# Shifting a few more edge chunks from GpSimd gathers to row-by-row loads in a graph layer

## The chip, the cores and the metric

The kernel runs on one core of one Trainium2 chip. The metric is device time in microseconds (us) of one execution. Three runs of the kernel before gave a median of 2628.38 us (2608.38 to 2629.09). One more execution was recorded by the hardware profiler; it took 1931.2 us. All views of the profile below belong to that one execution.

## What is computed

A graph network layer on 12,500 nodes with 128 features and 200,000 edges, sorted by destination. The reference, cut to what matters:

```python
h = jnp.maximum(_layernorm(x, axis=-1), 0.0)
msgs = h[src]
agg = jax.ops.segment_sum(msgs, dst, num_segments=n)
deg = jax.ops.segment_sum(jnp.ones((src.shape[0],)), dst, num_segments=n)
agg = agg / jnp.maximum(deg, 1.0)[:, None]
z = jax.nn.relu(agg @ Wg + h @ Ws + bg)
z = jnp.tanh(z @ W1 + b1)        # 128 -> 512
z = jnp.tanh(z @ W2 + b2)        # 512 -> 512
return x + z @ W3 + b3           # 512 -> 128
```

Everything is float32.

## The kernel before

**Setup (lines 132 to 323).** The normalised rows `h` are computed in pieces of up to 14 tiles of 128 nodes and written to a table `htab` in device memory (line 246). The edge indices are turned so that each edge chunk has a column.

**Chunks.** The edges are cut into 1563 chunks of 128. For each chunk the 128 source rows must lie in one SBUF tile of 128 x 128. `add` (line 432) then multiplies this tile with a one-hot matrix of the destinations (built on VectorE in groups of eight chunks, `onehot`, line 374), which adds the rows into a PSUM window of 144 nodes. Since the edges are sorted, chunk c falls around node 8c. There are three ways to get the rows of a chunk:

- 80 chunks are "raw": their rows of `x` are gathered by GpSimd during setup (line 153), before `htab` is complete, and normalised afterwards.
- 38 chunks are "slow" (the lists `slow_s` and `slow_a`, lines 86 to 100). Their rows are read from `htab` one at a time, 512 bytes each, by ordinary DMAs whose address comes from a register. 23 are read by SyncE (`srows`), 15 by ScalarE (`arows`). `row_loads` (line 337) first loads 32 addresses into registers (line 344, one table load per 32 rows) and then issues the 32 DMAs. The tiles come from the pool `rows_one`, with two buffers for each name.
- The remaining 1445 chunks are gathered from `htab` by GpSimd, one indirect DMA per chunk (`gather`, line 308), into 32 buffers (`AHEAD`).

**Blocks.** The nodes are cut into blocks of 512 (the last ones are smaller). When all chunks of a block have been added, its layers follow (`part0` to `part4`, lines 526 to 593): matmuls on TensorE, ReLU, Tanh and Identity on ScalarE. Each block needs the nodes' own rows transposed: `own` (line 480) loads 512 rows of `htab` into the tile `hb` (one buffer) on SyncE, `own_turned` (line 489) transposes them on TensorE and has ScalarE copy the result to `hT`. `own_part` (line 500) loads the block of `x` for the residual, and the finished block is stored, both on SyncE.

**What sets the order.** TensorE, ScalarE and SyncE keep the order in which the program issues their work (`keep_in_program_order`). The loop over the chunks (line 642) interleaves it: a chunk is added, then perhaps one step of a block's layers. Row loads are dealt out there by the number of chunks passed: SyncE gets a batch of 32 rows for each 32/128 of `EACH` = 58 chunks, ScalarE four rows for each 4/128 of `EACH_A` = 76 chunks. So ScalarE's row loads stand between its activations, and SyncE's stand between the loads of `hb` and `xb` and the stores of `o`. Every DMA of SyncE and ScalarE also takes the next of eight completion semaphores that both engines share, and waits for the DMA that had this semaphore before.

The lines of the loop that deal out row loads and own rows:

```python
batch = behind * P // (EACH * LOADS)
if behind > SLOW0 - 2 * EACH and batch > (behind - 1) * P // (EACH * LOADS):
    next(loading, 0)
...
if c % span == span - 52:
    own(c // span + 1)
if c % span == span - 10:
    own_turned(c // span + 1)
```

`span` is 64 chunks, one block. The functions that the diff touches:

Of the kernel before, what the change touches and what calls it, by code (L numbers as in the profile page):

```python
# [22 lines left out]
F32 = mybir.dt.float32  # L23
# [8 lines left out]
P = 128  # L32
EPS = 1e-5
CPR = 16
BLK = 512
# [3 lines left out]
RAW0 = 256  # L39
STEP = 40  # L40
AHEAD = 32
SLOW0 = 120
EACH = 58
EACH_A = 76
TOGETHER = 4
LOADS = 32
LATE = 12
LEAD = 10
QUICK = 1376
# [11 lines left out]
def windowed(ctx, tc, x, src, dst, Wg, Ws, bg, W1, b1, W2, b2, W3, b3, out, flag):  # L61
    nc = tc.nc
    N, D = x.shape
# [18 lines left out]
    def raw(c):  # L82
        return RAW0 <= c < RAW1 and (c - RAW0) % STEP < GRP


    slow_s, slow_a = [], []
    ns, na = 0, EACH // 2
    for c in range(SLOW0, NCH - 12):
        if raw(c):
            continue  # L90
        if ns <= 0:
            slow_s.append(c)
            ns = EACH
        elif na <= 0 and c < QUICK:
            slow_a.append(c)
            na = EACH_A
        else:
            ns -= 1
            na -= 1
# [20 lines left out]
    dram = ctx.enter_context(tc.tile_pool(name="dram", bufs=1, space=bass.MemoryType.DRAM))  # L120
    const = ctx.enter_context(tc.tile_pool(name="const", bufs=1))
    raws = ctx.enter_context(tc.tile_pool(name="raws", bufs=1))
    rows_one = ctx.enter_context(tc.tile_pool(name="rows_one", bufs=2))
    rows_in = ctx.enter_context(tc.tile_pool(name="rows_in", bufs=AHEAD))
    ps_c = ctx.enter_context(tc.tile_pool(name="ps_c", bufs=1, space=PSUM))
    ps_a = ctx.enter_context(tc.tile_pool(name="ps_a", bufs=2, space=PSUM))
# [55 lines left out]
    def centre(pool, xt, k, stats):  # L182
        nc.vector.tensor_reduce(stats[:, 0], xt, AX.X, ALU.add)
        nc.vector.scalar_tensor_tensor(xt, spread(stats[:, 0], k), -1.0 / D, xt, op0=ALU.mult, op1=ALU.add)
        sq = pool.tile([P, k, D], F32, name=f"sq{k}")
        nc.scalar.activation(sq, xt, AF.Square)
        nc.vector.tensor_reduce(stats[:, 1], sq, AX.X, ALU.add)

    def factors(stats):
        nc.scalar.activation(stats[:, 1], stats[:, 1], AF.Sqrt, bias=eps, scale=1.0 / D)  # L190
        nc.vector.reciprocal(stats[:, 1], stats[:, 1])
# [98 lines left out]
    ml = ctx.enter_context(tc.tile_pool(name="ml", bufs=2))  # L290
# [14 lines left out]
    def sp_dma(*a):  # L305
        tc.keep_in_program_order(nc.sync.dma_start(*a))  # L306

    def gather(c):
        r = rows_in.tile([P, D], F32, name="rows")
        nc.gpsimd.indirect_dma_start(  # L310
            out=r, out_offset=None, in_=htab,
            in_offset=bass.IndirectOffsetOnAxis(ap=scol[:, c : c + 1], axis=0),
        )
        rows_t[c] = r
# [40 lines left out]
    def raw_stats(i):  # L355
        return stats_raw[:, :, i * GRP : (i + 1) * GRP]

    def raw_scaled(i):
        h = raw_rows[i]
        scale(h, h, GRP, raw_stats(i))  # L360
        for j in range(GRP):
            rows_t[RAW0 + i * STEP + j] = h[:, j]
# [11 lines left out]
    def onehot(g):  # L374
        k = min(GRP, NCH - g * GRP)
        lo, w = window(g * GRP)
        is_raw = raw(g * GRP)
        oh = ed.tile([P, GRP, W_RAW], F32, name="ohr", bufs=2) if is_raw else oh_bufs[g % OHS]
        if not is_raw and w < oh_w[g % OHS]:
            nc.vector.memset(oh[:, :, w : oh_w[g % OHS]], 0.0)  # L380
            oh_w[g % OHS] = w
        nc.vector.tensor_tensor(  # L382
            oh[:, :k, :w], lane[:, None, :w].to_broadcast([P, k, w]),
            dloc[:, g * GRP : g * GRP + k][:, :, None].to_broadcast([P, k, w]), op=ALU.is_equal,
        )
        ohs[g] = oh
        step, n = (oh.shape[2], w) if is_raw else (PITCH - per, w + per * (k - 1))
        cnt = ed.tile([P, PITCH], BF16, name="cnt", bufs=16)
        part, row, col = oh.ap
        shifted = bass.AP(tensor=oh.tensor, offset=oh.offset, ap=[part, [col[0], n], [step * col[0], k]])  # L390
        with nc.allow_low_precision(reason="whole numbers up to the chunks of a group"):
            nc.vector.tensor_reduce(cnt[:, :n], shifted, AX.X, ALU.add)  # L392
        counts[g] = (lo, n, cnt)
# [10 lines left out]
    def count(b):  # L404

        n, m = blocks[b]
        dg = flat(ps_m.tile([P, 4, P], F32, name="pm"))
        groups = sorted({c // GRP for c in reach[b]})
        for g in groups:
            lo, w, cnt = counts[g]  # L410
            a0, a1 = max(lo, n), min(lo + w, n + m)
            pe.matmul(
                dg[:, a0 - n : a1 - n], ones, cnt[:, a0 - lo : a1 - lo], start=(g == groups[0]), stop=(g == groups[-1]),
                skip_group_check=True,
            )
        rd = ml.tile([P, BLK], F32, name="rd", bufs=3)
        nc.vector.tensor_scalar(rd[:, :m], dg[:, :m], 1.0, None, op0=ALU.max)  # L417
        nc.vector.tensor_reduce(total[:, b : b + 1], dg[:1, :m], AX.X, ALU.add)
        nc.vector.reciprocal(rd[:, :m], rd[:, :m])  # L419
        rds[b] = rd  # L420
# [59 lines left out]
    def own(s):  # L480

        n0 = s * BLK
        n = min(BLK, N - n0)
        k = -(-n // P)
        hb = ml.tile([P, BLK // P, D], F32, name="hb", bufs=1)
        sp_dma(hb[:, :k], htab[n0 : n0 + k * P, :].rearrange("(t p) d -> p t d", p=P))
        owns[s] = hb

    def own_turned(s):

        k = -(-min(BLK, N - s * BLK) // P)
        hb = owns.pop(s)
        pt = ps_t.tile([P, BLK // P, P], F32, name="pt")
        for t in range(k):
            pe.transpose(pt[:, t, :], hb[:, t, :], ident)
        hT = ml.tile([P, BLK], F32, name="hT")
        act.copy(hT[:, : k * P], pt[:, :k, :].rearrange("p t n -> p (t n)"))
        hTs[s] = hT
# [116 lines left out]
    work, done, nxt, behind = [], 0, 0, 0  # L615
    ngrp = -(-NCH // GRP)
    span = BLK // per
    now = at = 0

    def store(upto):  # L620
        while stores and stores[0][0] <= upto:
            sp_dma(*stores.pop(0)[1:])
# [5 lines left out]
    def go_on(w):  # L628
        nonlocal now
        if w:  # L630
# [3 lines left out]
            if w[1] is None:  # L634
                work.remove(w)

    own(0)
    own_turned(0)
    onehot(0)
    onehot(1)  # L640
    counted = 0
    for c in range(NCH):
        g = c // GRP
        at = c
        store(c if c >= QUICK else c - LATE)
        if c % GRP == 0 and g + 2 < ngrp:
            onehot(g + 2)
            if raw((g + 2) * GRP):
                raw_scaled(((g + 2) * GRP - RAW0) // STEP)
            if 2 <= g < 2 + NRAW:  # L650
                centre(ed, raw_rows[g - 2], GRP, raw_stats(g - 2))
            if g == 2 + NRAW:
                factors(stats_raw)

        while c % GRP == GRP // 2 and counted < len(blocks) and reach[counted][-1] // GRP <= g + 1:
            count(counted)
            counted += 1
        while nxt < len(order) and nxt < behind + AHEAD:
            gather(order[nxt])
            nxt += 1  # L660
        if not raw(c) and c not in slow:
            behind += 1
            batch = behind * P // (EACH * LOADS)
            if behind > SLOW0 - 2 * EACH and batch > (behind - 1) * P // (EACH * LOADS):
                next(loading, 0)
            batch = behind * P // (EACH_A * TOGETHER)
            if behind > 48 and batch > (behind - 1) * P // (EACH_A * TOGETHER):
                next(loading_a, 0)
        if c >= QUICK:

            there = 7.5 + 1.251 * (NRAW * GRP + order.index(c)) if c not in slow else 0
            while soonest() and max(now, soonest()[2]) < there:
                go_on(soonest())
            now = max(now, there) + 0.27
        add(c)

        lead = LEAD if c < QUICK else 2
        if done < len(blocks) and (c - lead if across[done] else c) >= reach[done][-1]:
            if across[done]:
                merge(done)  # L680
            quick = reach[done][-1] + LEAD >= QUICK

            before = done - 1 if done and reach[done - 1][-1] + LEAD < QUICK else None
            work.append([layers(done, before), 0, 0, 0, quick and blocks[done][1] <= P])
            done += 1
        if (c // span + 1) * BLK < N:
            if c % span == span - 52:
                own(c // span + 1)
            if c % span == span - 10:
                own_turned(c // span + 1)  # L690
        if c < QUICK:
            if c % 2 == 0:
                go_on(work[0] if work else None)
        if c == QUICK:
            for b, (_, n) in enumerate(blocks):
                if n < BLK:
                    own_part(b)
# [379 lines left out]
```

## Time and profile before

| What | Value |
|---|---|
| Median of three runs | 2628.38 us (2608.38 to 2629.09) |
| Profiled execution | 1931.2 us |
| Its span, first to last instruction | 1928.7 us |
| What lies around the span | 2.5 us |
| TensorE matmul busy | 1299.0 us (67%), granted clock 0.866 |
| VectorE busy | 1066.8 us (55%) |
| ScalarE busy, without DMA issue | 228.1 us (12%) |
| GpSimd busy | 1442.0 us (75%) |
| DMA engines | 0.2 to 0.3 of their time after setup, 72 GB/s on average |

The profiled execution is 697 us shorter than the median of the runs. The profile can't show why; it is one execution, and each of its durations is taken as it stands.

How to read the profile: a row of a group names the line, the engine, the operation and the tiles it writes and reads ("out<-in"), the number of instructions, busy time, mean nanoseconds of one, and the idle time of the engine just before them with what ended most of it. A row of the waits names who waited for whom, the total in us, how many times, and the longest. A row of the timeline has a start, a duration and the number of merged instructions; in brackets the idle time before. "SPq" and "ACTq" are DMAs being issued by SyncE and ScalarE; issuing is not counted as busy. "Issue" is time in which nothing shown was waited for.

### The profile page before, as it was taken

Reading aid. Unit: us, or ns where it says so; the run is one execution under the profiler, and the core shown is the slowest. Engines: PE = TensorE matmul, PEld = TensorE weight load, DVE = VectorE, ACT = ScalarE, POOL = GpSimd, SP = SyncE. Lnnn points to the kernel's source line nnn. Section 1 sums busy time; section 2 is a strip of 40 time slices with the busy share of each in tenths; the row PEclk is TensorE's granted clock in tenths of the full one; section 3 lists DMA queues with packets and bytes.
Section 4 is the critical chain, followed back from the end, with each engine's and each line's share of the span. In section 5 each row is a group of like instructions: output and inputs, shape, how many; then the busy total and the mean of one; then the engine's idle time right before and its main releaser. Section 6 shows DMA issues by size and latency. Waiting matters only on the chain.

```text
span 1928.7 us, 24991 instructions
## 1 busy us (share of the span) xinstructions
PE 1299.0 (67%) x5212; PEld 819.1 (42%) x5212; DVE 1066.8 (55%) x651; ACT 228.1 (12%) x362; POOL 1442.0 (75%) x1533
## 2 busy tenths in 40 slices
PE   0056487775757678758775676566776746878787
PEld 0034354443535445534443344344443424554466
DVE  7964865555556856636544465354554536645430
ACT  1100111010101111111100110001101101101122
POOL 7777777777777777777777777777777777777774
PEclk9999688898878888888887898878988879879698
DMA  8822222222222222222222222222222222222221
GB/s 202 233 65 53 55 67 59 61 71 60 67 71 66 66 70 67 71 71 61 65 61 66 71 61 65 61 71 66 61 66 66 61 70 61 71 78 71 66 62 40
DMA packets 128692, 139.69 MB, mean 72 GB/s; under 512 B 35036, under 2 KB 103294, under 8 KB 128336
## 3 DMA queue, kind: packets, MB, share of 16 engines
q0 software_dynamic: 48800, 100.04, 20.5%
q1 hardware_dynamic: 72654, 33.65, 6.4%
q10 hardware_dynamic: 7076, 4.32, 0.9%
q14 instruction: 119, 0.97, 0.2%
q8 instruction: 43, 0.70, 0.2%
HBM read 125.07 MB, written 12.82 MB: 71 GB/s over the span
## 4 chain that ended last, share of the span: by engine, by line
DMA 31%; PE 28%; issue 17%; SPq 11%; DVE 5%; POOL 3%; ACTq 3%; ACT 1%; POOLq 0%; DVEq 0%
PE pm L297 16%; DMA rows<-htab,scol 16%; SPq L306 10%; PE agg L297 6%; DMA arows<-htab 5%; PE edge L297 4%; DMA srows<-htab 4%; POOL rows L310 3%; DMA hb<-htab 3%; ACTq L335 3%; DVE cnt L392 2%; DMA xt<-in_x_dram 2%; PE pt L300 1%; DVE oh L382 1%; SPq L344 1%
## 5 line engine op out<-in xcount | busy, mean ns | idle before, releaser
L310 POOL DMA_INDIRECT rows<-htab,scol x1445 | 1363.4, 944 | 440.8 <-issue 258.9
L297 PE MATMUL pm<-h,w 128*128 128x512 f32 (+4 forms) x1344 | 649.1, 580 | 26.3 <-ACT h L329 26.3
L297 PE MATMUL agg<-oh,rows 128*128 128x144 f32 (+3 forms) x2068 | 484.4, 342 | 219.9 <-DMA rows<-htab,scol 217.1
L297 PEld LDWEIGHTS agg<-oh,rows 128*128 128x128 f32 x2068 | 360.7, 215 | 530.1 <-DMA rows<-htab,scol 395.2
L382 DVE TENSOR_TENSOR oh<-shared,dloc 128x1152 f32<-128x1152 f32 (+2 forms) x186 | 243.4, 1314 | 605.8 <-PE edge L297 354.9
L392 DVE TENSOR_REDUCE cnt<-oh 128x200 bf16<-128x1600 f32 (+2 forms) x186 | 525.8, 2832 | 5.4
L297 PEld LDWEIGHTS pm<-h,w 128*128 128x128 f32 x1344 | 223.4, 206 | 42.2 <-ACT h L329 29.4
L297 PEld LDWEIGHTS edge<-oh,rows 128*128 128x128 f32 x822 | 150.3, 219 | 160.5 <-issue 85.8
L297 PE MATMUL edge<-oh,rows 128*128 128x144 f32 (+2 forms) x822 | 181.8, 333 | 39.7 <-DMA rows<-htab,scol 39.4
L300 PE MATMUL pt<-ident,hb 128*128 128x128 f32 x98 | 24.5, 398 | 242.7 <-DMA hb<-htab 242.7
L329 ACT ACTIVATE h<-pm,b2c 128x512 f32<-128x512 f32 (+4 forms) x112 | 70.8, 632 | 447.6 <-PE pm L297 229.3
L300 PEld LDWEIGHTS pt<-ident,hb 128*128 128x128 f32 x98 | 16.8, 204 | 246.3 <-issue 246.3
L153 POOL DMA_INDIRECT raw<-in_x_dram,rsrc x80 | 77.7, 971 | 25.4 <-issue 23.8
L329 ACT ACTIVATE h<-pm,b1c 128x512 f32<-128x512 f32 (+4 forms) x112 | 69.9, 632 | 203.2 <-PE pm L297 107.3
L419 DVE RECIPROCAL rd<-rd 128x512 f32<-128x512 f32 (+4 forms) x28 | 81.8, 2920 | 0.0
L332 ACT COPY hT<-pt 128x512 f32<-128x512 f32 (+1 forms) x25 | 14.4, 577 | 410.2 <-PE pt L300 383.9
L589 DVE TENSOR_TENSOR o<-pt,xb 128x512 f32<-128x512 f32 x23 | 15.8, 688 | 75.9 <-PE pt L300 75.9
L417 DVE TENSOR_SCALAR rd<-pm 128x512 f32<-128x512 f32 (+4 forms) x28 | 17.2, 616 | 63.1 <-PE pm L297 63.1
L212 PE MATMUL pm<-ident,idx_f 98*128 98x98 f32 x32 | 6.2, 376 | 62.0 <-DVE idx_f L208 55.7
L297 PE MATMUL pm<-mT,wg 128*128 128x512 f32 (+4 forms) x56 | 32.6, 669 | 22.7 <-DVE mT L533 22.5
L329 ACT ACTIVATE h<-pm,bgc 128x512 f32<-128x512 f32 (+4 forms) x28 | 17.7, 632 | 240.0 <-PE pm L297 144.1
L297 PE MATMUL pm<-hT,ws 128*128 128x512 f32 (+4 forms) x56 | 34.8, 711 | 0.0
(72 smaller groups left out, 496.9 us busy)
## 6 DMA issues: line engine op xcount, KB each, us to landing
srows<-htab SPq DMA_DIRECT2D x2944, 0.5 KB
arows<-htab ACTq DMA_DIRECT2D x1920, 0.5 KB
rows<-htab,scol POOLq DMA_INDIRECT x1445
hb<-htab SPq DMA_DIRECT2D x24, 256.0 KB
xb<-in_x_dram SPq DMA_DIRECT2D x23, 256.0 KB
out_dram<-o SPq DMA_DIRECT2D x23, 256.0 KB
htab<-h SPq DMA_DIRECT2D x6, 896.0 KB
xt<-in_x_dram SPq DMA_DIRECT2D x5, 896.0 KB
```

Of the source, the lines that this page charges most:

```text
L153: nc.gpsimd.indirect_dma_start(out=t[:, j, :], out_offset=None, in_=x, in_offset=bass.IndirectOffsetOnAxis(ap=rsrc[:, g, j : j + 1], axis=0),)
L297: tc.keep_in_program_order(nc.tensor.matmul(*a, **k))
L300: tc.keep_in_program_order(nc.tensor.transpose(*a, **k))
L306: tc.keep_in_program_order(nc.sync.dma_start(*a))
L310: nc.gpsimd.indirect_dma_start(out=r, out_offset=None, in_=htab, in_offset=bass.IndirectOffsetOnAxis(ap=scol[:, c : c + 1], axis=0),)
L329: tc.keep_in_program_order(nc.scalar.activation(*a, **k))
L335: tc.keep_in_program_order(nc.scalar.dma_start(*a))
L344: loads, vs = nc.values_load_multi_w_load_instructions(place[i : i + 1, p0 : p0 + LOADS], engines=[engine], min_val=0, max_val=(N - 1) * ROWB,
L382: nc.vector.tensor_tensor(oh[:, :k, :w], lane[:, None, :w].to_broadcast([P, k, w]), dloc[:, g * GRP : g * GRP + k][:, :, None].to_broadcas ...
L392: nc.vector.tensor_reduce(cnt[:, :n], shifted, AX.X, ALU.add)
L417: nc.vector.tensor_scalar(rd[:, :m], dg[:, :m], 1.0, None, op0=ALU.max)
L419: nc.vector.reciprocal(rd[:, :m], rd[:, :m])
```

## The change

The sync engine reads the rows of 27 chunks instead of 23 and ScalarE those of 19 instead of 15; GpSimd gathers 1437 chunks instead of 1445. Each of the two has four row buffers instead of two. The first slow chunk is chunk 160 instead of 120, and SyncE's batches are dealt out so that a chunk is read up to three intervals of 48 ahead instead of two of 58. ScalarE's last slow chunk may lie up to 60 chunks behind `QUICK`. The tile `hb` has two buffers; the load for a block is issued right after the transposes of the block before it, a whole block (64 chunks) ahead of its own transposes instead of 42 chunks. Setup reads the indices of 46 slow chunks (`at_i`, line 321) instead of 38.

```diff
-SLOW0 = 120
-EACH = 58
-EACH_A = 76
+SLOW0 = 160
+EACH = 48
+EACH_A = 60
...
-        elif na <= 0 and c < QUICK:
+        elif na <= 0 and c < QUICK + EACH_A:
...
-    rows_one = ctx.enter_context(tc.tile_pool(name="rows_one", bufs=2))
+    rows_one = ctx.enter_context(tc.tile_pool(name="rows_one", bufs=4))
...
-        hb = ml.tile([P, BLK // P, D], F32, name="hb", bufs=1)
+        hb = ml.tile([P, BLK // P, D], F32, name="hb", bufs=2)
...
     own(0)
+    own(1)
     own_turned(0)
...
-            if behind > SLOW0 - 2 * EACH and batch > (behind - 1) * P // (EACH * LOADS):
+            if behind > SLOW0 - 3 * EACH and batch > (behind - 1) * P // (EACH * LOADS):
...
-        if (c // span + 1) * BLK < N:
-            if c % span == span - 52:
-                own(c // span + 1)
-            if c % span == span - 10:
-                own_turned(c // span + 1)
+
+        if c % span == span - 10 and (c // span + 1) * BLK < N:
+            own_turned(c // span + 1)
+            if (c // span + 2) * BLK < N:
+                own(c // span + 2)
```

## The prediction

> **What bounds the kernel now.** I read the page's busy times first, then the groups of GpSimd, its waits and the end of its timeline, then the waits of SyncE, the two row tiles, and the tile `hb`.
>
> GpSimd is the busiest engine by share, and its busy digits are flat. The group of the gathers and the waits of GpSimd:
>
> ```profile
> PE 1299.0 (67%) x5212; PEld 819.1 (42%) x5212; DVE 1066.8 (55%) x651; ACT 228.1 (12%) x362; POOL 1442.0 (75%) x1533
> POOL 7777777777777777777777777777777777777774
> L310 POOL DMA_INDIRECT rows<-htab,scol x1445 | 1363.4, 944 | 440.8 <-issue 258.9
> L153 POOL DMA_INDIRECT raw<-in_x_dram,rsrc x80 | 77.7, 971 | 25.4 <-issue 23.8
> ...
> POOL rows L310 <- issue: 258.9, 849, 0.3
> POOL rows L310 <- PE agg L297: 79.0, 259, 0.3
> ```
>
> The reader is to see that no idle piece before a gather is longer than 0.3 us, whoever is named as its releaser. So GpSimd never waits; 0.944 + 0.305 = 1.249 us is its fixed period, from the first raw gather to the last. The tile view has the first table gather at 105.0 us and the last at 1908.0: 1803.0 / 1444 = 1.249 us. Setup is hidden too: the 80 raw gathers run on the same beat until the table gathers begin. So the profiled span is about 4 us, 1525 gathers of 1.249 us (1905 us), and 20 us of layers of the last block. GpSimd bounds the profiled execution from end to end.
>
> Next come the engines the change loads. The tiles of the row loads, SyncE's waits, and two stretches of SyncE's timeline (one late, when ScalarE has no rows left, one in the middle):
>
> ```profile
> L306 SPq DMA_DIRECT2D srows<-htab x2944: 224/228/387, 103.5 to 1788.8; - x197
> L335 ACTq DMA_DIRECT2D arows<-htab x1920: 227/228/520, 166.2 to 1605.7; - x192
> L344 SPq TENSOR_LOAD <-place x92: 2058/2157/2910, 101.3 to 1775.9; - x92
> ...
> SPq L306 <- DMA arows<-htab: 397.1, 270, 40.0
> ...
> 1734.89 25.98 SPq L306 DMA_DIRECT2D srows<-htab  x65
> 1765.55 23.44 SPq L306 DMA_DIRECT2D srows<-htab  x64
> 1789.09 0.42 SPq L306 DMA_DIRECT2D out_dram<-o  x1
> ...
> 1194.87 37.65 SPq L306 DMA_DIRECT2D srows<-htab  x64
> 1238.08 24.16 SPq L306 DMA_DIRECT2D srows<-htab  x64
> 1270.07 1.86 SPq L306 DMA_DIRECT2D srows<-htab  x4
> ```
>
> SyncE spends 1788.8 - 103.5 = 1685.3 us on 23 chunks, 73.3 us each; its due interval is 58 x 1.249 = 72.4 us. Left alone it needs 1789.1 - 1734.9 = 54.2 us for a chunk with its table loads and block DMAs; in the middle one took 75.2 us (1194.87 to 1270.07). The difference is interference: 397.1 us of waiting for ScalarE's row loads, since both share eight semaphores and ScalarE stands at activations.
>
> Last, the tile `hb`, and one of the places where TensorE waits for it:
>
> ```profile
>   DMA hb<-htab: 242.7, 19
> ...
> 1265.48 1.09 PE L300 MATMUL pt<-ident,hb 128*128 128x128 f32 x4 [22.10 <-DMA hb<-htab]
> ```
>
> TensorE stood 242.7 us for `hb`, 12.8 us each time, because SyncE issued the load late. GpSimd didn't feel it: 32 row buffers are 32 x 1.249 = 40 us of cover.
>
> **The change part by part**, against the profiled 1931.2 us.
>
> *Fewer gathers.* 1445 to 1437: 8 x 1.249 = -10.0 us on the bounding engine. This is the only part on the path. A rule speaks against it: the Trainium skill ("DMA: Bandwidth & Descriptors", section "Issuing engines are not separate DMA queues") says that starting DMAs from several engines saves only the sequencer's time to start them, usually small beside the transfer. By the rule the sum is 0. Here the row decides: the DMA engines are a quarter busy, and the 1.249 us are the issuing engine's time. I take -10.0.
>
> *SyncE, 4 chunks more.* 512 row DMAs and 16 table loads; 27 chunks must fit one per 48 x 1.249 = 60.0 us. Its pace isn't known when ScalarE is busier. From below: 54.2 us, left alone. From above: 73.3, today's mean, which includes waits that came from being paced by the rest. Two stretches of 32 loads in the middle took 12.4 and 14.9 us, 10 us a chunk apart, so contention brings 54.2 to 64 at most where no long wait is met. I take 62 (an estimate), nearer to the free end, because `hb` no longer closes a circle (SyncE late, `hb` late, TensorE late, ScalarE's copy late, SyncE waiting for ScalarE's semaphore). The last slow chunk, 1533, is due after 1437 gathers, at 105 + 1437 x 1.249 = 1900 us. SyncE is through at 103.5 + 27 x 62 = 1778: hidden, with 122 us over. At 66.5 us a chunk the cover is gone; each us above costs 27 us. Table loads are a large share of the pace: the skill (same page, "Latency and other measured facts") has a floor of about 600 ns for one, the row 2157. By the page the four loads of a chunk would take 2.4 us and the pace would be 56; by the row they take 8.6. I use the row.
>
> *ScalarE, 4 chunks more.* One chunk per 60 x 1.249 = 74.9 us. A stretch of 12 loads took 4.91 us, 0.41 each: 128 x 0.41 = 52.5, four table loads of about 2.2 us 8.8, and its 228.1 us of compute spread over 1900 us another 9.0: 70.3 of 74.9. Hidden. Queued behind its loads are the activations that TensorE's next layer waits for; behind those the chunk adds; behind those, after 40 us, GpSimd.
>
> *Four buffers, earlier reading, earlier `hb`.* A SyncE chunk in the built order now has its last row 4 to 70 chunk adds before its use, before 1 to 33; `hb` gets 64 chunks of notice instead of 42. That removes the 242.7 us of TensorE idle, worth 0 while GpSimd has its cover, and up to 242.7 if it hasn't. New waits: a row tile for the chunk four before it, `hb` for the transposes two blocks back, both long done.
>
> *Setup.* Eight more index loads on ScalarE (some 0.3 us each, 2.4 us) and one more `hb` load on SyncE (0.4 us). Hidden under the raw gathers.
>
> Sum: 1931.2 - 10.0 = 1921.2 us, 0.52% less. The runs' median is 697 us above the profiled execution. Scaled (2628.38 / 1931.2 = 1.361), the gain is 13.6 us; shifted, 10. I predict 2615 us. About 1% is what a measurement of this kernel can tell from no change (its three runs lie 0.8% apart).
>
> **The rivals.** They live in the 697 us.
>
> *Row loads are the bound (slower).* SyncE is paced at 73.3 us against 72.4 due, so it has nothing to spare in the middle. If the 697 us are slower row loads, they are 697 / 4864 = 0.143 us a row, and 1024 more rows cost 147 us: 2628 + 147 = 2775. In the profiled execution the same rival means a SyncE pace above 66.5 us; at 73.3 it ends 103.5 + 27 x 73.3 = 2083 plus the tail. For it: SyncE's waits, and the interval cut by 17% without any cheaper load. Against it: SyncE runs a chunk in 54 us when free, and a slower GpSimd would give it more time.
>
> *The waits for `hb` are exposed (faster).* If TensorE lags more in the timed runs, the cover of 40 us is used up and each of 25 blocks passes its wait to GpSimd; 697 / 25 = 28 us a block is the size of the longest waits seen. The earlier `hb` then saves about half of 242.7, with the 13.6: 2628 - 121 - 14 = 2493. For it: the waits are real and the change removes their cause. Against it: GpSimd shows no trace of them, and when TensorE is slower SyncE is less late.
>
> *GpSimd alone is slower in the timed runs (the main case).* 697 / 1525 = 0.457 us a gather, period 1.706; 8 of them are 13.6 us, and SyncE's interval stretches to 82 us, which hides it fully. The runs' closeness (2628.38 and 2629.09) suits a fixed beat.
>
> **How the numbers follow.** Main case 0.43, between 2600 and 2640, 2615 the likeliest. Row loads 0.33, from 2660 to 2900. `hb` exposed 0.24, from 2390 to 2595. Leaving about 1 in 10 on each side: 2490 to 2790. So faster by over 1%: 0.24; within 1%: 0.43; slower by over 1%: 0.33.
>
> **What would show it.** Right: GpSimd still without a wait over 0.3 us, 1437 gathers at 1.249, last one near 1898 us; TensorE's waits for `hb` nearly gone; SyncE's first-to-last row divided by 27 at 60 to 66. Wrong: GpSimd waiting for TensorE by more than 0.3 us; TensorE waiting for `srows` or for ScalarE's `h`; SyncE's pace over 66.5 us. The time itself is wrong if what makes the runs longer than the profile weighs on SyncE and ScalarE rather than on GpSimd.

## The result, and the profile after

| Kernel | Median, us | Runs, us |
|---|---|---|
| before | 2626.61 | 4 runs, 2608.38 to 2629.09 |
| changed | 2778.41 | 4 runs, 2771.82 to 2799.80 |

The ratio is 1.061 (95% interval 1.053 to 1.068): the change makes the kernel about 6% slower. The profiled execution of the changed kernel took 2780.86 us (span 2778.6), so this time the profile and the runs agree.

The kernel before takes about 1930 us in some sets of runs and about 2620 to 2650 us in others, and the profile shown ahead of the prediction was of the short kind, the timed runs of the long one. Below, "at 1930" and "at 2630" name the kind, and a ratio always compares a kernel with the kernel before in its own set.

The page of the changed kernel, the same lines as before:

```profile
PE 1321.2 (48%) x5212; PEld 886.9 (32%) x5212; DVE 1068.0 (38%) x651; ACT 228.0 (8%) x362; POOL 1437.0 (52%) x1525
POOL 7666456554555444555526454364544545346261
L310 POOL DMA_INDIRECT rows<-htab,scol x1437 | 1358.6, 945 | 1266.1 <-PE edge L297 441.5
L300 PE MATMUL pt<-ident,hb 128*128 128x128 f32 x98 | 25.9, 409 | 543.2 <-DMA hb<-htab 480.3
```

A gather still takes 0.945 us, but GpSimd is no longer steady: most of its digits lie at 4 to 6 (7 all along before), and the idle time before the gathers grew from 440.8 to 1266.1 us. Its waits and TensorE's:

```profile
POOL rows L310 <- PE edge L297: 441.5, 75, 43.9
POOL rows L310 <- issue: 332.3, 1043, 3.4
POOL rows L310 <- PE agg L297: 283.9, 141, 19.4
...
PE pt L300 <- DMA hb<-htab: 480.3, 19, 45.1
PE pm L297 <- ACT h L329: 244.3, 37, 16.8
```

GpSimd waits up to 43.9 us for TensorE to free a row buffer, and TensorE waits up to 45.1 us for `hb`: 480.3 us in all, twice the 242.7 us of before, although the load now stands a whole block ahead in the program. One of these places, first SyncE's timeline, then TensorE's (start, duration, what, and in brackets the idle time before):

```profile
1545.56 19.40 SPq L306 DMA_DIRECT2D srows<-htab  x41
1565.06 0.41 SPq L306 DMA_DIRECT2D hb<-htab  x1
```

```profile
1568.33 1.09 PE L300 MATMUL pt<-ident,hb 128*128 128x128 f32 x4 [21.16 <-DMA hb<-htab]
1569.20 1.06 PE L297 MATMUL pm<-h,w 128*128 128x512 f32 x1
```

`hb` is issued 0.1 us after the last of a run of row loads and used 3.3 us later. SyncE issued it as soon as its queue came to it: the queue is behind. The tile view of the rows says how far:

```profile
L306 SPq MOVE srows<-htab x3456: 1/29/1400, 117.0 to 2654.3; - x192
L306 SPq DMA_DIRECT2D srows<-htab x3456: 2/228/1406, 117.0 to 2654.4; - x192
```

A row is a register MOVE and a DMA. 27 chunks take 2654.4 - 117.0 = 2537.4 us, 94.0 each; the prediction had 62. The columns min/median/max tell a second thing: single MOVEs here take up to 1400 ns. In the profile of before all took 29:

```profile
L306 SPq MOVE srows<-htab x2944: 29/29/29, 103.4 to 1788.7; - x197
```

Where the 700 us between the two kinds of sets lie is seen in a profile of the kernel before at 2630 (e18 below, span 2630.0), its groups and SyncE's rows:

```profile
L310 POOL DMA_INDIRECT rows<-htab,scol x1445 | 1364.4, 944 | 1113.1 <-PE edge L297 365.5
L300 PE MATMUL pt<-ident,hb 128*128 128x128 f32 x98 | 26.1, 412 | 501.3 <-DMA hb<-htab 473.8
```

```profile
L306 SPq MOVE srows<-htab x2944: 1/29/1422, 116.8 to 2531.4; - x197
L306 SPq DMA_DIRECT2D srows<-htab x2944: 2/228/1414, 116.8 to 2532.1; - x197
```

The gathers are as fast as ever (0.944 us). SyncE's 23 chunks take 2532.1 - 116.8 = 2415.3 us instead of 1685.3, that is 730 us more, and the span is 701 us longer; GpSimd stands idle for 1113.1 us before its gathers and TensorE 473.8 us for `hb`. TensorE's granted clock is lower too (0.757, before 0.866), but its matmuls are busy for 1320.5 us instead of 1299.0, which is 21.5 of the 701. So the trace says that at 2630 the kernel before is already held up by SyncE's row loads; the runs with fewer chunks and with cheaper loads (e11, e10) bear on this, though both are variants of the changed kernel.

One thing does not fit a queue that simply runs at its own speed: SyncE takes 2415.3 / 23 = 105.0 us a chunk here and 94.0 in the changed kernel. Why a row is slower in the kernel before is not known.

### The profile page after: what moved, and what is told of

The parts are those of the page before. It is cut to its first block, busy times and chain, and to the rows that moved or that the text cites. A ratio compares the mean times of both kernels' runs of the same rounds, so it can differ in the third digit from the quotient of the medians.

```text
span 2778.6 us, 27033 instructions
## 1 busy us (share of the span) xinstructions
PE 1321.2 (48%) x5212; PEld 886.9 (32%) x5212; DVE 1068.0 (38%) x651; ACT 228.0 (8%) x362; POOL 1437.0 (52%) x1525
## 5 line engine op out<-in xcount | busy, mean ns | idle before, releaser
L310 POOL DMA_INDIRECT rows<-htab,scol x1437 | 1358.6, 945 | 1266.1 <-PE edge L297 441.5
L297 PE MATMUL pm<-h,w 128*128 128x512 f32 (+4 forms) x1344 | 732.0, 644 | 442.9 <-ACT h L329 237.1
L297 PEld LDWEIGHTS agg<-oh,rows 128*128 128x128 f32 x2070 | 395.1, 236 | 323.4 <-issue 291.4
L297 PE MATMUL agg<-oh,rows 128*128 128x144 f32 (+3 forms) x2070 | 423.5, 336 | 76.0 <-issue 52.0
L297 PEld LDWEIGHTS pm<-h,w 128*128 128x128 f32 x1344 | 246.7, 226 | 478.2 <-ACT h L329 247.1
L300 PE MATMUL pt<-ident,hb 128*128 128x128 f32 x98 | 25.9, 409 | 543.2 <-DMA hb<-htab 480.3
L297 PE MATMUL edge<-oh,rows 128*128 128x144 f32 (+2 forms) x804 | 158.8, 316 | 16.9 <-issue 12.5
L297 PE MATMUL pm<-mT,wg 128*128 128x512 f32 (+4 forms) x56 | 42.0, 843 | 143.8 <-DVE mT L533 91.5
L297 PE MATMUL agg<-sums,ident 128*128 128x140 f32 (+4 forms) x108 | 25.3, 370 | 121.9 <-ACT sums L332 78.2
L297 PEld LDWEIGHTS agg<-sums,ident 128*128 128x128 f32 x108 | 19.2, 243 | 126.2 <-ACT sums L332 79.8
L297 PEld LDWEIGHTS pm<-mT,wg 128*128 128x128 f32 x56 | 11.7, 259 | 148.1 <-DVE mT L533 94.2
```

What stands on the lines that cost most here:

```text
L297: tc.keep_in_program_order(nc.tensor.matmul(*a, **k))
L300: tc.keep_in_program_order(nc.tensor.transpose(*a, **k))
L310: nc.gpsimd.indirect_dma_start(out=r, out_offset=None, in_=htab, in_offset=bass.IndirectOffsetOnAxis(ap=scol[:, c : c + 1], axis=0),)
```

## The experiments

Theories. *The queue*: SyncE issues in order and has no time to spare; more rows make everything behind them late (rows, `hb`, `xb`, stores), and GpSimd stops through TensorE. *H*: only `hb` is late, and an earlier place in the program would cure it. *ScalarE*: its activations stand behind its row loads, and TensorE waits for them. *Buffers*: four buffers and the new read distance do the harm. *GpSimd*: the long sets are long because GpSimd is slower there; the profile of e18 and the 0.945 us above had already spoken against it. Each ratio is to the kernel before in the same set, with its 95% interval.

### At 1930: which part does it

**The kernel before again (e1), and a third time (e12).** No edit. They give the measurement's own error.

> The kernel before, unchanged, profiled once more. Theory A (in its usual runs the row loads of SyncE and ScalarE are issued slowly, as in the changed kernel's trace, where both engines take steps of about 0.70 us an instruction): about 2627 us, GpSimd waiting for TensorE by some 600 to 700 us, SyncE near 100 us a chunk, steps of 0.70 us in its timeline. Theory B (GpSimd's own gathers are slower in the usual runs): about 2627 us, gathers 1.7 us apart and no wait of GpSimd over 0.3 us. Theory C (the median is not the same state as any profiled execution): the profile shows 1931 us again.

> The kernel before once more, for a trace where it takes 2620 us. If it takes 2620 here, theory S: SyncE's row loads, with steps of 0.70 us an instruction, run at about 104 us a chunk, (2618 - 97 - 117) / 23, first row near 117 and last near 2520, and GpSimd waits some 650 us for TensorE. If GpSimd never waits there and its gathers lie 1.7 us apart, theory S falls. If it takes 1932 here, it repeats the first look.

Measured: 1932.49 us, ratio 1.0004 (0.9995 to 1.0013), and 1930.22, ratio 1.0003 (0.9994 to 1.0012). So 0.3% can be told apart in these sets.

**The change again (e5).** No edit to the changed kernel.

> The changed kernel, unchanged. Theory S (SyncE's and ScalarE's own pace of row loads is the bound once it passes 66.5 us a SyncE chunk): if the kernel before takes 1932 us here, this takes 1921 (pace under 66.5) to 2024 us (no better than the counts alone); if the kernel before takes 2627 us here, this takes 2778 us, with instructions of SyncE in steps of 0.70 us. Theory G (GpSimd alone decides): 0.5% less in both cases, which the first result already speaks against.

Measured: 2027.01 us against 1930.3, ratio 1.051 (1.049 to 1.053). The change costs 5.1% here and 6.1% at 2630, so what makes the long sets long is not needed for the loss. Its waits (SyncE's last) and SyncE's rows:

```profile
PE pt L300 <- DMA hb<-htab: 389.0, 19, 37.4
PE pm L297 <- ACT h L329: 143.1, 44, 12.2
...
POOL rows L310 <- PE edge L297: 131.4, 115, 17.3
...
SPq L306 <- DMA arows<-htab: 299.5, 256, 41.9
SPq L306 <- DMA srows<-htab: 75.8, 265, 0.6
```

```profile
L306 SPq MOVE srows<-htab x3456: 29/29/29, 99.4 to 1920.9; - x192
L306 SPq DMA_DIRECT2D srows<-htab x3456: 224/228/312, 99.5 to 1920.9; - x192
```

No MOVE is stretched, and the picture is still that of the result: 1821.4 / 27 = 67.5 us a chunk, TensorE late for `hb`, GpSimd late for TensorE. Between 1200 and 1600 us, 778 rows were issued, 65.8 us a chunk, and only 9.5 us of the 400 were pauses of over 1 us outside table loads: SyncE has no time to spare. Counted in the trace, the 400 us are 252 of rows at their free distance (0.32 us each), 49 of small delays between rows, 89 around table loads, 9.5 of pauses. That is not all its own work: in this stretch SyncE stood 52.5 us for ScalarE's row loads and 21.6 us for its own earlier ones, through the shared semaphores. Over the whole run the two rows above give (299.5 + 75.8) / 27 = 13.9 us a chunk, and with the 54.2 us of a chunk left alone 68.1, close to the 67.5. The same sum fits the kernel before: (397.1 + 52.2) / 23 = 19.5, and 54.2 + 19.5 = 73.7 against 73.3. So at 1930 the pace is SyncE's own instructions plus waits at semaphores that it shares with ScalarE. A kernel in which the two share none was not tried.

The end of the run, SyncE's timeline:

```profile
1880.85 0.41 SPq L306 DMA_DIRECT2D hb<-htab  x1
1883.57 23.34 SPq L306 DMA_DIRECT2D srows<-htab  x64
1906.96 0.40 SPq L306 DMA_DIRECT2D xb<-in_x_dram  x1
1907.46 0.45 SPq L306 DMA_DIRECT2D out_dram<-o  x1
1910.81 10.34 SPq L306 DMA_DIRECT2D srows<-htab  x32
1921.24 0.41 SPq L306 DMA_DIRECT2D out_dram<-o  x1
1921.74 0.46 SPq L306 DMA_DIRECT2D hb<-htab  x1
```

The rows end at 1920.9 and the span at 2018.0: 97 us follow. In them GpSimd still gathers, until 1994.0 (59 gathers of 1.249 us are 73 us), and then comes the last block. The last row stands that far from the end in the program's order, and all that shares its queue with it.

**The counts alone (e2).** The kernel before with the new counts, old buffers, old place of `hb`; a chunk is still read two intervals ahead, which are now of 48 instead of 58:

```diff
-EACH = 58
-EACH_A = 76
+EACH = 48
+EACH_A = 60
...
-        elif na <= 0 and c < QUICK:
+        elif na <= 0 and c < QUICK + EACH_A:
...
+    slow_s, slow_a = slow_s[:27], slow_a[:19]
```

> The kernel before with 27 and 19 slow chunks, but two row buffers, the old reading distance and one hb buffer. Theory A (cost by rows): 1024 rows more cost what the change cost, 2780 us or, if the buffers and the earlier hb helped against it, 2800 to 2900. Theory B': the read-ahead and the buffers did the harm: near 2627.

Measured: 2023.91 us, ratio 1.048 (1.046 to 1.050): 92 of the 97 us of e5. TensorE's waits:

```profile
PE pt L301 <- DMA hb<-htab: 284.2, 16, 28.8
PE agg L298 <- DMA srows<-htab: 120.2, 9, 24.7
```

Here TensorE also waits for the rows themselves. In e5, which differs in read distance, row buffers and `hb`, the last row of a chunk is issued 18 to 92 us before its use, and the wait for `hb` is longer instead. The lateness has moved from the rows to `hb`; the loss stays.

**Buffers and early `hb` alone (e3, e15).** The changed kernel with the counts of before. With `SLOW0` and `EACH` of before, the batches of rows also fall on the same chunks as before, so the longer read distance is not in this run:

```diff
-SLOW0 = 160
-EACH = 48
-EACH_A = 60
+SLOW0 = 120
+EACH = 58
+EACH_A = 76
...
-        elif na <= 0 and c < QUICK + EACH_A:
+        elif na <= 0 and c < QUICK:
```

> The changed kernel with the counts of before (23 and 15): four buffers, reading further ahead, two hb buffers. Theory A: no more rows, so 2627 us or a little less (to 2550) since hb comes early. Theory B': the buffers and the order did the harm, so near 2780.

> Four row buffers, earlier reading and two hb buffers with the counts of before (23 and 15), once more. Where the kernel before takes 2620 us: at a pace of 95 us a chunk 2400 us, at the pace of the kernel before (104) 2620. If the kernel before takes 1932 here: 1931 again.

Measured: 1931.11 us, ratio 0.9998 (0.9989 to 1.0006), and 1929.48, ratio 0.9994 (0.9985 to 1.0002). Nothing. TensorE's wait for `hb` fell from 242.7 us to

```profile
  DMA hb<-htab: 114.8, 14
```

and that was worth nothing, because GpSimd's cover of 40 us had hidden it. *Buffers* falls at 1930: here are the buffers without the loss, and in e2 the loss without the buffers and without the longer read distance.

**SyncE's four chunks without ScalarE's (e6), and ScalarE's without SyncE's (e7, e13).** Edits to the changed kernel:

```diff
 # e6: 27 and 15
-EACH_A = 60
+EACH_A = 76
-        elif na <= 0 and c < QUICK + EACH_A:
+        elif na <= 0 and c < QUICK:
 # e7, e13: 23 and 19
-SLOW0 = 160
-EACH = 48
+SLOW0 = 120
+EACH = 58
-        elif na <= 0 and c < QUICK + EACH_A:
+        elif na <= 0 and c < QUICK + EACH_A // 2:
```

> The changed kernel with ScalarE's count of before: 27 chunks by SyncE, 15 by ScalarE. Theory S with SyncE as the slower queue: close to the changed kernel, within 10 us of it. Theory S with the sum of both queues' rows as the limit: half of the added rows, so about half of its difference to before.

> The changed kernel with SyncE's count of before: 23 chunks by SyncE, 19 by ScalarE. Theory S with SyncE as the slower queue: close to the kernel before, at most 10 us above it where that takes 1932 us. With the sum of the rows as the limit: about half of the changed kernel's difference to before.

> 23 chunks by SyncE and 19 by ScalarE with the four buffers and the early hb, once more. Where the kernel before takes 2620 us: theory S with SyncE's pace of 95 us a chunk, as in the runs with 25 and 27: 117 + 23 x 95 + 97 = 2400 us. If the kernel before takes 1932 here: 1925 again.

Measured: e6 2019.89 us, ratio 1.047 (1.045 to 1.050). e7 1924.82 us, ratio 0.9971 (0.9961 to 0.9982), and again 1924.82, ratio 0.9976 (0.9969 to 0.9983). The waits of e7, GpSimd's, TensorE's and SyncE's:

```profile
POOL rows L310 <- issue: 262.3, 860, 0.3
POOL rows L310 <- DMA rows<-htab,scol: 63.9, 209, 0.3
...
PE pt L300 <- DMA hb<-htab: 32.4, 1, 32.4
PE pm L297 <- ACT h L329: 31.5, 11, 13.6
...
SPq L306 <- DMA arows<-htab: 304.3, 266, 41.6
```

SyncE's four chunks are nearly the whole loss (+90 of 97 us); ScalarE's four gain the four gathers they save (4 x 1.249 = 5.0; measured 5.5 and 5.3). The early `hb` does here what it was meant to: one wait is left, and GpSimd never waits for more than 0.3 us. 23 chunks alone don't do it: e3 has them too, with ScalarE's old spacing, and 114.8 us of waits for `hb`; its SyncE stood 400.0 us for ScalarE's row loads, in e7 304.3. Why was not taken apart. *ScalarE* falls at 1930. e7 is the fastest version at 1930, ahead of the kernel before by 0.2 to 0.3%; e6 and e7 were not run at 2630.

**No row loads (e4), and half of them (e8, e14).** e4 is the kernel before with empty slow lists (all 1563 chunks are raw or gathered, and setup reads no row indices). e8 and e14 are the changed kernel with 12 and 8 chunks:

```diff
 # e4
+    slow_s, slow_a = [], []
 # e8, e14
-EACH = 48
-EACH_A = 60
+EACH = 110
+EACH_A = 150
```

> The kernel before without slow chunks: GpSimd gathers all 1483 chunks that are not raw. Theory A: GpSimd is the bound again at 1.249 us a gather: 1563 x 1.249 + 24 = 1976 us, 25% less than before. Theory B (slower gathers, 1.706 us): 2690 us.

> The changed kernel with 12 chunks by SyncE and 8 by ScalarE (2560 rows instead of 5888), GpSimd gathers 1463. Theory S: GpSimd is the bound again on any chip, (80 + 1463) x 1.249 + 24 = 1951 us; where the kernel before takes 2627 us this would be 26% faster. If what makes 2627 us lies elsewhere than in the row loads, it stays above 2500 us there.

> 12 chunks by SyncE and 8 by ScalarE, once more. Where the kernel before takes 2620 us: theory S: 12 x 95 us is less than what GpSimd takes, so GpSimd is the bound, 1951 to 2000 us, some 25% less than before. If it stays above 2500, the row loads don't make the 2620. If the kernel before takes 1932 here: 1951 again.

Measured: e4 1979.60 us, ratio 1.025 (1.023 to 1.027); e8 1951.05, ratio 1.011 (1.009 to 1.013), and again 1951.46, the same ratio. 38 more gathers cost 47.9 us, 1.26 each; 18 more cost 20.8, 1.15 each. While SyncE keeps up, a gather more or less is worth about its period of 1.249 us. Neither was run at 2630.

### At 2630: is it `hb`, or the queue

**`hb` two blocks ahead (e9, e16).** The changed kernel with three buffers for `hb`; the tile `cnt` gives up one of its 16 buffers for the room:

```diff
-        hb = ml.tile([P, BLK // P, D], F32, name="hb", bufs=2)
+        hb = ml.tile([P, BLK // P, D], F32, name="hb", bufs=3)
...
     own(1)
+    own(2)
...
-            if (c // span + 2) * BLK < N:
-                own(c // span + 2)
+            if (c // span + 3) * BLK < N:
+                own(c // span + 3)
```

> The changed kernel with three hb buffers, the load of a block issued two blocks (128 chunks) ahead instead of one; the counts of VectorE have 15 buffers instead of 16 to make room. In the changed kernel's trace TensorE stood 389 us for hb while each slow chunk's last row was issued 18 to 92 us before its use. Theory H (SyncE runs late at 66 us a chunk, but only hb, queued behind the rows, is late for TensorE): the waits for hb vanish and the rows' own slack is used up: 1921 to 1945 us where the kernel before takes 1930. Theory S alone (the pace of the rows is the bound, whatever stands late first): the wait moves from hb to the rows, 2000 us or more.

> The changed kernel with hb loaded two blocks ahead, once more, for where the kernel before takes 1931 us. Theory H (only hb, queued behind the rows on SyncE, is late for TensorE; the rows have slack at their use): 1921 to 1945 us. Theory S alone (SyncE's pace of 66 us a chunk is the bound, whatever stands late first): 2000 us or more. Where the kernel before takes 2620 it repeats 2772.

Measured: 2772.51 us against 2618.36, ratio 1.059 (1.053 to 1.066); again 2814.90 against 2647.71, ratio 1.064 (1.059 to 1.070). As slow as the change. After the first block `hb` is now issued 41 us or more before its transposes, and TensorE stands at the same place as before. The waits of e9, VectorE's and TensorE's:

```profile
DVE o L589 <- DMA xb<-in_x_dram: 293.4, 14, 65.1
...
PE pt L300 <- issue: 288.0, 17, 66.9
PE agg L297 <- DMA srows<-htab: 198.0, 8, 33.6
```

TensorE's row names only "issue", so the releaser has to be found by time. Around one such wait, the timelines of SyncE, VectorE and TensorE:

```profile
1354.53 32.00 SPq L306 DMA_DIRECT2D srows<-htab  x60
1386.59 0.41 SPq L306 DMA_DIRECT2D xb<-in_x_dram  x1
```

```profile
1389.30 0.69 DVE L589 TENSOR_TENSOR o<-pt,xb 128x512 f32<-128x512 f32 x1 [25.14 <-DMA xb<-in_x_dram]
```

```profile
1390.10 1.09 PE L300 MATMUL pt<-ident,hb 128*128 128x128 f32 x4 [31.22 <-issue]
```

The load of `xb` came out from behind 60 rows, VectorE's last step of a block waited for it, and 0.1 us after that step the transposes began, which write the tile `pt` that it reads. The next transfer in SyncE's queue had taken the place of `hb`, and behind it the rows (198.0 us). SyncE's rows again take (2658.2 - 120.3) / 27 = 94.0 us a chunk, as in the changed kernel:

```profile
L306 SPq DMA_DIRECT2D srows<-htab x3456: 1/228/1444, 120.3 to 2658.2; - x192
```

*H* falls at 2630; at 1930 it was not tried.

**25 chunks on SyncE (e11, e17).** The kernel of e9 with another spacing, 25 and 19 chunks:

```diff
-SLOW0 = 160
-EACH = 48
+SLOW0 = 150
+EACH = 53
```

> The kernel of the run with hb two blocks ahead, with an interval of 53 for SyncE: 25 chunks by SyncE, 19 by ScalarE, 1439 gathers. SyncE's pace of 66 us a chunk is just the due interval of 53 x 1.249 = 66.2 us. Theory S: just hidden, 1525 - 1519 = 6 gathers less than before, 1923 us where the kernel before takes 1930 (up to 1935 if the pace is a little over). If it is over 1960, the break-even lies at a slower interval than the pace says.

> 25 chunks by SyncE and 19 by ScalarE with hb two blocks ahead, once more, for where the kernel before takes 1931 us. SyncE's measured 66 us a chunk against 66.2 us due: 1923 us, up to 1935. If it is over 1960, the break-even lies at a slower interval than the pace says. Where the kernel before takes 2620 it repeats 2598.

Measured: 2598.49 us, ratio 0.993 (0.991 to 0.995); again 2626.92, ratio 0.992 (0.990 to 0.994). Two chunks fewer than e9 save (2772.5 - 2598.5) / 2 = 87 us each. SyncE's pace in e11 was (2500.1 - 117.7) / 25 = 95.3 us a chunk:

```profile
L306 SPq DMA_DIRECT2D srows<-htab x3200: 2/228/1408, 117.7 to 2500.1; - x189
```

So between these two kernels a chunk on SyncE costs nearly its pace. Both runs beat the kernel before at 2630 by 0.7 to 0.8%, though SyncE has 25 chunks and not 23: a chunk takes it 95.3 us instead of 105.0. They also have more chunks on ScalarE and an early `hb`; which of these gives the gain was not taken apart.

**Fixed addresses (e10).** The changed kernel with row addresses known when it is built: it loads no addresses and reads fixed rows of the table instead of the edges' source rows, everything else is done. A row is then one instruction, without MOVE and table loads:

```diff
-                loads, vs = nc.values_load_multi_w_load_instructions(
...
-                for p, v in enumerate(vs, p0):
-                    dma(rb[p : p + 1, :], hbytes[bass.ds(v, ROWB)].rearrange("(o b) -> o b", o=1))
+                for p in range(p0, p0 + LOADS):
+                    v = (c * 8 + p * 61) % N * ROWB
+                    dma(rb[p : p + 1, :], hbytes[v : v + ROWB].rearrange("(o b) -> o b", o=1))
```

> The changed kernel with the same 5888 row loads from addresses fixed when the program is built: no table loads (108 of 2.16 us on SyncE, 76 of 2.29 on ScalarE) and no register per row, so the rows loaded are not those of the edges and the sums are not the reference's. Theory S with SyncE's own issue time as the limit: a chunk falls from 66 us to 128 x 0.26 + 2, some 40 us, GpSimd is the bound again, 1921 us where the kernel before takes 1930. If the limit is in the DMAs' landing or in the shared semaphores, the table loads and registers cost little, and it stays above 1990.

Measured: 2362.43 us, ratio 0.904 (0.898 to 0.910). SyncE's rows:

```profile
L306 SPq DMA_DIRECT2D srows<-htab x3456: 2/247/1478, 114.8 to 2210.1; - x192
```

77.6 us a chunk instead of 94.0: as many transfers of the same size, 410 us faster than e9. So much of the cost is in the instructions that issue, not in the transfers. ScalarE's loads lost their MOVEs and table loads too; what each engine's share of the 410 us is was not separated. The hoped-for 40 us a chunk were not reached: DMAs are still stretched, so the register MOVE is not what brings the stretching, and TensorE still waits 217.4 us for `hb`.

**The kernel before at 2630 (e18).** No edit; for its profile.

> The kernel before once more, for its trace where it takes 2620 us. Theory S: SyncE at about 104 us a chunk with instructions in steps of 0.70 us, GpSimd waiting some 650 us for TensorE. If GpSimd never waits, with gathers 1.7 us apart, theory S falls there. Where it takes 1931 us, nothing new.

Measured: 2641.23 us against 2647.71, ratio 0.999 (0.997 to 1.002). Its profile is read above.

## Why the prediction was wrong

The forecast was 2615 us, about 0.5% less; the time was 2778.41. The first rival, row loads as the bound, gave 2775. The step that failed shows already at 1930, where the change costs 5.1% (e5); the 697 us, taken up below, are a second error on top of it.

**SyncE's pace, the step that failed.** "I take 62" was too low, and "hidden, with 122 us over" did not hold: a chunk takes 65.8 us in the middle of e5 at 1930, 67.5 over the whole run, and 94.0 at 2630. The estimate started from a chunk at the end of the run, when ScalarE had no rows left (54.2 us), and allowed 10 us for contention "at most", of which it took 8. The 10 were the difference between two stretches of 32 loads, a sample of two. The term that was too small is this contention: e5 has 13.9 us a chunk of waits at the shared semaphores. At 2630 these waits are fewer ((136.6 + 54.3) / 27 = 7.1 us a chunk in the changed kernel), and the rows themselves are longer by the steps of the last section. The reason given for staying low, that "`hb` no longer closes a circle", brought nothing: in e3, with the early `hb`, SyncE's 23 chunks took 1700.9 us (1685.3 before), and in e5 TensorE waited longer for `hb`, not less.

**The due time was set at the wrong place.** The prediction asked when the last row is used (1900 us) and got a break-even of 66.5 us. By that, 67.5 us a chunk would cost 27 us; e5 is 97 above the kernel before. With a longer read distance the rows are early, but the loads of `hb` and `xb` stand behind them in the same queue, and these have their own due times. Read off e5, 97 us of work follow the last row, so it would have to be issued by 1921.2 - 97 = 1824 us: (1824 - 99.5) / 27 = 63.9 us a chunk. That figure comes from the run it explains; a kernel at that pace was not tried at 1930.

**"Removes the 242.7 us of TensorE idle": the opposite.** 389.0 us at 1930, 480.3 at 2630. An earlier place in the program brings a load in time only if its queue is not behind: with 23 chunks on SyncE and 19 on ScalarE 32.4 us were left (e7), with 23 and 15 114.8 (e3). That such a cut is worth 0 while GpSimd has its cover was right (e3).

**The 697 us.** The main case put them on GpSimd ("period 1.706"). The gathers take 0.944 and 0.945 us at 2630, and some 600 of SyncE's 730 extra us lie in steps between its own instructions (last section). The scaled sum, "SyncE's interval stretches to 82 us, which hides it fully", fell with it: SyncE was what stretched. The closeness of the runs was no evidence for GpSimd's beat: those of e2, where SyncE is behind, lie as close together (2022.81 to 2025.41).

**The rival's number was nearly right, in part by luck.** It spread the 697 us over the rows of both engines (0.143 us a row x 1024 = 147). The runs put them on SyncE: 730 / 2944 = 0.248 us a row more than at 1930. The 148.6 us between the spans of e18 and the changed kernel (two sets) divide so: 23 chunks took 2415.3 us and 27 took 2537.4, 122 more, and after the last row 124.2 us follow instead of 97.9, 26 more. But four chunks at 94.0 us are 376, not 122: the other 23 chunks became 11 us faster each (94.0 instead of 105.0). The rival knew of neither, and why the pace differs stays open.

**What was right.** A gather is worth about its period while GpSimd sets the time (e4, e8, e7). ScalarE's four chunks are hidden at 1930 (e7; e5 is only 7 us above e6), and so is the setup (first row of SyncE at 99.5 us, before 103.5). The prediction weighed two rules against rows. The Trainium skill ("DMA: Bandwidth & Descriptors", section "Issuing engines are not separate DMA queues") calls the sequencer's time to start a DMA usually small beside the transfer; at 2630 that time decides, as e10 shows with 410 us for as many transfers of the same size. And for a table load the row of 2157 ns was the better guide than the floor of some 600 ns (same page, "Latency and other measured facts"): with the floor the estimate of the pace would have been 56 us, still further from 67.5.

## What to carry to other kernels

A queue that issues in order has one pace and many due times: ask of each item in it (here rows, `hb`, `xb`, stores) when its place in the program is reached, not only when the last row is used, and reckon with the mean pace under load rather than the free one, waits at shared semaphores included. When an engine has no time to spare, moving one late load earlier only shows the next one; take work off the engine. If the profiled execution and the timed runs differ by a quarter, get the profile of the long kind before forecasting: the bound can be another engine there.

## What the hardware showed that was not expected

At 2630, the instructions of SyncE and, less, of ScalarE come in steps of 0.70 us. In the profile of the kernel before at 2630 (e18), 415 neighbouring SyncE rows start about 0.70 us apart (0.65 to 0.75) and 422 about 1.40 (1.30 to 1.50), over the whole run; these 837 distances sum to 899 us, where 0.32 us each would be 268, so 631 are extra. In the profile at 1930 the same count gives 85 distances, 59 us in all and 32 extra. The difference is some 600 of the 730 us by which SyncE's rows are longer. ScalarE has 171 such distances (188 us) at 2630. The MOVEs longer than 0.1 us are 633 of SyncE's 2944 at 2630, and none at 1930. Instructions of GpSimd keep their durations. In e10, where each row is one instruction, the steps remain (900 distances of 0.70 or 1.40 us). What makes these two engines take such steps in some sets of runs, and why one chip showed both kinds in sets a quarter of an hour apart, stays open: no run here varied anything that switched it.
